# One array for the scan's h in place of two tiles, and the variance's clamp on VectorE

## The chip, the cores and the metric

The kernel runs on one core of a Trainium2 chip. The metric is the device time of one execution in microseconds (us). The engines are named as the profile names them: PE is TensorE, DVE is VectorE, ACT is ScalarE, POOL is GpSimd and SP is SyncE, which here only starts transfers.

## The reference

Eight images of 128 × 128 positions with 128 channels pass through two layers. Layer 0 is a linear attention block with a layer norm and a residual. Layer 1 projects to 2 × 256 channels (xb and z), runs a depthwise 3 × 3 convolution and a silu on xb, and then a selective scan with one state over the 16384 positions in four directions. What the change touches is the scan and the normalization behind it:

```python
delta = softplus(dt + dbias)                  # per channel and position
x_c   = exp(delta * A) * x_c + delta * u * Bt # the scan over positions
y     = x_c * Ct (+ u * D)                    # four directions are summed
yz    = (y0 + y1 + y2 + y3) * silu(z)
mu    = yz.mean(-1); xc = yz - mu
var   = (xc * xc).mean(-1)                    # over the 256 channels
out   = (gamma * xc / sqrt(var + 1e-05) + beta) @ Wout
```

## The kernel before, in words

The program has three stages: layer 0, the front of layer 1 (projection, convolution, the x projection), and the scan stage `layer1_scan`, which starts behind a barrier of all engines (L773). The change lies in the scan stage.

**Units.** The 256 channels lie as two halves c of 128 partitions. A scan of 16384 positions is cut in 16 chunks of 1024 (CH). A `Slot` is one direction of one output image; its number in the image is its *place*, 0 to 3. Eight images of four slots of 16 chunks make 512 units n = 0 to 511, and they run in that order. The sum of the directions, y, is one array in SBUF of 128 KB per partition.

**One unit.** PE makes delta's argument in PSUM (`delta`), ACT takes its softplus into `sp` (`soften`, L938) and the exponential into PSUM (`decay`, L942). POOL multiplies u by sp into h (`weigh`, L951, one for each half). DVE scans h in place (`scan`, L959 and L961), starting from the last column of the same half of the unit before. In the next step DVE multiplies h by the position's C, which PE has spread over the partitions in PSUM: `emit` writes y itself at place 0 (L979); at the other places it writes one 512-position half to PSUM (L989, L993), which `gather` (L1001) adds to y on DVE, and the other in place in h (L982), which `add` (L1009) adds to y on POOL.

**The buffers of h.** `weigh(n, 0)` takes a new tile of two halves from a pool with two buffers:

```python
hs[n] = wp.tile([P, NC2, CH], F32, name="h", bufs=2)
```

A new tile may be written only when everything that reads or writes the tile before it in that buffer, that of unit n − 2, is done. That takes in the second scan of unit n − 1, since `scan(n − 1, 1)` reads its starting column in h of unit n − 2.

**A leaving image.** When the four slots of image o are summed, its 16 pieces leave during the 16 units of place 0 of image o + 1 (after image 7, in 16 further steps without scans). I call these units *tails*. For a piece m: `gate` multiplies y by z (L1029; its half 1 on DVE where a piece left in the step before too, its half 0 on POOL); ACT squares it; PE sums both over the channels (`moments`), ACT copies the sums (`keep`), PE turns them to tokens (`to_tokens`), ACT squares the mean (`square_mean`, L1058); DVE subtracts (`variance`, L1062); POOL clamps and adds epsilon (`deviation`, L1066) and takes the power −1/2 (L1067), all on tiles of 128 × 8; PE multiplies the gated piece by Wout (`project`, L1074); DVE scales the product into r in eight instructions (`store`, L1080); and SP starts r's transfer to the output. Parts of the sum that came by way of DRAM are accumulated into y by transfers that POOL starts (`add_d`, L907, 1 MB each).

**What sets the order.** Within the stage each engine's instructions stand in the order in which `step(n)` (L1105 to L1189) issues them; `in_order` fixes it. Semaphores between the engines come from the tiles: who wrote and who read which region. In `step(n)`, the order on DVE is: emit and emit of unit n − 1, with the gate of half 1 between them, scan(n, 0), the store, scan(n, 1), variance. On POOL it is: weigh(n, 0), deviation, weigh(n, 1), the gate of half 0, add, add_d.

**Setup of the scan stage.** The weights of delta are split in three bf16 parts by `split3` (three casts and two subtractions on DVE) and written to DRAM, from where `Slot.weights` loads them for each slot in turn. The parts lie in a tile `w16` that borrows the buffers of h (tag "h", L782 to L794). It runs once for the weights (8 partitions) and once for the bias (1 partition).

Of the kernel before, what the change touches and what calls it, by code (L numbers as in the profile page):

```python
# [8 lines left out]
F32 = mybir.dt.float32  # L9
BF16 = mybir.dt.bfloat16  # L10
AF = mybir.ActivationFunctionType
ALU = mybir.AluOpType
# [4 lines left out]
P = 128  # L17
# [4 lines left out]
NC2 = 2  # L22
R = 8
K = 4
# [6 lines left out]
CH = 1024  # L31
# [3 lines left out]
EPS1 = 1e-5  # L35
# [5 lines left out]
def split3(eng, parts, x):  # L41

    for j in range(3):
        eng.tensor_copy(parts[j], x)
        if j < 2:
            eng.tensor_tensor(x, x, parts[j], ALU.subtract)
# [701 lines left out]
def layer1_scan(ctx: ExitStack, tc, ubs, xps, zs, gs, dtw, dtb, a_log, gamma, beta, w_out, out):  # L748
# [15 lines left out]
    nc = tc.nc  # L764
    const = ctx.enter_context(tc.tile_pool(name="l2c", bufs=1))
    big = ctx.enter_context(tc.tile_pool(name="l2b", bufs=1))
    wp = ctx.enter_context(tc.tile_pool(name="l2w", bufs=3))
# [14 lines left out]
    D2 = 2 * P  # L782
    wparts = dram.tile([3, R, K, D2], BF16, name="wparts")
    bparts = dram.tile([3, K, D2], BF16, name="bparts")
    for dst, src, rows in ((wparts, dtw.rearrange("k r d -> r k d"), R), (bparts, dtb.rearrange("o (k d) -> o k d", d=D2), 1)):
        x = wp.tile([rows, K, D2], F32, name="w32", tag="sp", bufs=2)
        nc.sync.dma_start(x, src)
        q = wp.tile([rows, 3, K, D2], BF16, name="w16", tag="h", bufs=2)
        split3(nc.vector, [q[:, j] for j in range(3)], x)
        for j in range(3):  # L790
            if rows == 1:
                nc.sync.dma_start(dst[j : j + 1], q[:, j])
            else:
                nc.sync.dma_start(dst[j], q[:, j])  # L794

# [49 lines left out]
        nc.vector.tensor_tensor(wg[:, c, :], wg[:, c, :], pb, ALU.subtract)  # L847

    y = big.tile([P, NC2, L], F32, name="y")
    yturn = y.rearrange("p c (w h) -> p c h w", h=H)  # L850

    class Slot:
# [49 lines left out]
    ubt, sp, da, hs = {}, {}, {}, {}  # L902
# [40 lines left out]

    def weigh(n, c):
        if c == 0:
            hs[n] = wp.tile([P, NC2, CH], F32, name="h", bufs=2)
        u, t, h = ubt.pop((n, c)), sp.pop((n, c)), hs[n][:, c, :]
        if units[n][0].permuted:
            u = u.rearrange("p (e h w) -> p h e w", e=2, w=W // 2)
            t, h = (v.rearrange("p (h e w) -> p h e w", e=2, w=W // 2) for v in (t, h))  # L950
        nc.gpsimd.tensor_tensor(h, u, t, ALU.mult)  # L951
# [108 lines left out]
    def variance(m):  # L1060
        rst[m] = rstd = sm.tile([P, GW, NC2], F32, name="rstd")
        nc.vector.tensor_tensor(rstd, pts.pop(m)[:, :, :, 1], mv.pop(m), ALU.subtract)  # L1062

    def deviation(m):
        rstd = rst[m]
        nc.gpsimd.tensor_scalar(rstd, rstd, 0.0, EPS1, ALU.max, ALU.add)  # L1066
        nc.gpsimd.tensor_tensor(rstd, rstd, half, ALU.pow)  # L1067

    def project(m, hf, bank):
# [20 lines left out]
    for o in range(B):  # L1090
        n = (o + 1) * K * NCH
# [13 lines left out]
    def step(n):  # L1105
# [22 lines left out]
        if live:  # L1128
            decay(n, 1)
            weigh(n, 0)  # L1130
            if n + 2 < N:
                load(n + 2, 0)
        if last:
            deviation(last[1])
        if live:
            weigh(n, 1)
            if n + 2 < N:
                load(n + 2, 1)
# [24 lines left out]
        if now:  # L1163
            variance(now[1])
# [42 lines left out]
@with_exitstack  # L1207
def tile_kernel(ctx: ExitStack, tc, a, out):
    dram = ctx.enter_context(tc.tile_pool(name="dram", bufs=1, space=DRAM))
    x1 = dram.tile([B, P, L], F32, name="x1")  # L1210
    ubs = dram.tile([B, 2, NC2, P, L], F32, name="ubs")
    xds = dram.tile([B, R + 2, L], F32, name="xds")
    xps = dram.tile([B, 2, 3, R + 2, L], BF16, name="xps")
    zs = dram.tile([B, NC2, P, L], F32, name="zs")
    gs = dram.tile([2, NC2, P, L], F32, name="gs")
    layer0(
        tc, a["x"], a["L0_conv_w_qkv"], a["L0_conv_w_out"], a["L0_conv_b_out"],
        a["L0_conv_gamma"], a["L0_conv_beta"], a["L1_conv_Win"], x1, zs,
    )
    layer1_front(  # L1220
        tc, x1, a["L1_conv_Win"], a["L1_conv_conv_w"], a["L1_conv_conv_b"], a["L1_conv_Wxproj"],
        a["L1_conv_D_param"], ubs, xds, xps, gs,
    )
    layer1_scan(
        tc, ubs, xps, zs, gs, a["L1_conv_dt_weight"], a["L1_conv_dt_bias"], a["L1_conv_A_log"],
        a["L1_conv_gamma"], a["L1_conv_beta"], a["L1_conv_Wout"], out,
    )
# [40 lines left out]
```

## Time and profile before

| | us |
|---|---|
| median of 3 executions (lowest, highest) | 9282.05 (9277.97, 9287.36) |
| the profiled execution | 9288.8 |
| its span, to which the profile refers | 9287.0 |
| scan stage: barrier, first scan, last scan | 4498.6, 4528.4, 9141.9 |
| busy in the span: DVE, POOL, ACT, PE | 7986.4, 7316.7, 7097.3, 6364.4 |
| busy on POOL in the scan stage: weigh L951, add L1009, gate L1029 | 2416.6, 1159.4, 329.7 |
| clamp L1066 and power L1067 on POOL, 128 each | 143.3, 212.9 |
| variance L1062 on DVE, 128 | 18.6 |

The profile is one execution. A group of instructions is a line, an engine, an operation and its operands (the names of the program, with shape and type), then how many there are, their busy time, the mean of one in ns, and the idle time in front of them with what ended most of it. A line of the timeline is start, duration, engine, line and operation; several alike in a row are taken together, and brackets hold the idle time ahead of it and what released it. Durations overlap a little at both ends: the next instruction can start some 0.06 to 0.1 us before the end of the one before it on its engine. A wait is put down to what came last.

### The profile page before, as it was taken

How to read it: one execution, taken by the hardware profiler on the slowest of the kernel's cores; microseconds unless marked ns; L12 is line 12 of the kernel's file. 1: busy time of each engine (PE TensorE's matmuls, PEld its weight loads, DVE VectorE, ACT ScalarE, POOL GpSimd, SP SyncE). 2: the span in 40 equal slices, each digit the busy share in tenths (PEclk: the TensorE clock that was granted, in tenths of full speed). 3: DMA queues.
4: the chain of work that ended last, by engine and by line, in shares of the span. 5: the costliest groups of instructions: out<-in, count | busy, mean ns of one | idle time of the engine just before them, and what ended most of it. 6: DMA issues, size and time to landing. Idle time of an engine off the chain costs nothing.

```text
span 9287.0 us, 91371 instructions
## 1 busy us (share of the span) xinstructions
PE 6364.4 (69%) x24512; PEld 3119.9 (34%) x24512; DVE 7986.4 (86%) x7953; ACT 7097.3 (76%) x8066; POOL 7316.7 (79%) x4684
## 2 busy tenths in 40 slices
PE   8899998988899999999334636346363463643636
PEld 5555555554333333333102304113041140311403
DVE  6667666774799999999799999999999999999996
ACT  5555555658789999999687787888888878888784
POOL 3446444564689988888599899999999989999897
PEclk9999999999999999999555657557575575755757
DMA  1322333223478788888658659577594775957757
GB/s 76 145 84 97 135 120 145 80 100 136 153 247 249 253 244 244 245 245 243 200 156 226 209 180 261 155 222 227 175 269 154 220 221 169 269 161 208 234 167 214
DMA packets 934770, 1750.67 MB, mean 189 GB/s; under 512 B 150228, under 2 KB 376148, under 8 KB 926064
## 3 DMA queue, kind: packets, MB, share of 16 engines
q1 hardware_dynamic: 873328, 1509.92, 48.0%
q0 software_dynamic: 60928, 234.90, 13.6%
q8 instruction: 200, 3.28, 0.1%
q14 instruction: 314, 2.57, 0.1%
HBM read 1052.36 MB, written 692.12 MB: 188 GB/s over the span
## 4 chain that ended last, share of the span: by engine, by line
DVE 36%; PE 5%; DMA 3%; issue 3%; POOL 2%; ACT 1%; DVEq 0%; SPq 0%; POOLq 0%; ACTq 0%
DVE h L961 10%; DVE h L959 10%; DVE y L1001 4%; DVE h L982 4%; DVE px L989 3%; PE px L1074 3%; DMA out<-r 3%; DVE r L1080 2%; DVE px L993 1%; POOL h L951 1%; PE pm L1042 1%; PE pq L1054 0%; PE pc L967 0%; POOL y L1009 0%; POOL z L1029 0%
## 5 line engine op out<-in xcount | busy, mean ns | idle before, releaser
L951 POOL TENSOR_TENSOR h<-ubt,sp 128x1024 f32<-128x1024 f32 x1024 | 2416.6, 2389 | 374.9 <-DMA rows<-xps 92.6
L934 PE MATMUL px<-rows,dtw 128*128 128x512 bf16 x2048 | 956.3, 566 | 2277.8 <-DVE y L1001 1073.2
L534 DVE SCALAR_TENSOR_TENSOR acc<-xb,cw,acc 128x1024 f32<-128x1024 f32 x1024 | 1320.3, 1289 | 133.6 <-ACT xb L502 89.8
L526 POOL TENSOR_TENSOR tap<-tap 128x1024 f32<-128x1024 f32 x512 | 1223.6, 2393 | 243.7 <-ACT tap L524 220.4
L938 ACT ACTIVATE sp<-px 128x1024 f32<-128x1024 f32 x1024 | 1046.7, 1024 | 436.4 <-PE px L934 413.8
L934 PEld LDWEIGHTS <-dtw 128*128 128x128 bf16 x2048 | 168.8, 110 | 3100.8 <-issue 1031.3
L961 DVE TENSOR_TENSOR_SCAN h<-px,h 128x1024 f32<-128x1024 f32 x512 | 1177.4, 2331 | 31.6 <-ACT px L942 15.4
L959 DVE TENSOR_TENSOR_SCAN h<-px,h 128x1024 f32<-128x1024 f32 x512 | 1178.1, 2330 | 22.4 <-POOL h L951 18.5
L1009 POOL TENSOR_TENSOR y<-y,h 128x512 f32<-128x512 f32 x768 | 1159.4, 1553 | 4.3 <-DVE h L982 4.3
L942 ACT ACTIVATE px<-sp,sa 128x1024 f32<-128x1024 f32 x1024 | 1110.4, 1109 | 6.1
L515 PE MATMUL acc<-xi,wt 128*128 128x512 f32 x2048 | 937.6, 600 | 53.6 <-ACT ures L539 53.6
L524 ACT ACTIVATE tap<-xb,cw 128x1024 f32<-128x1024 f32 x768 | 837.3, 1139 | 15.2 <-POOL xb L499 15.1
L282 POOL TENSOR_TENSOR q<-q,qs 128x512 f32<-128x512 f32 x256 | 271.6, 1061 | 697.0 <-DVE qs L281 697.0
L938 ACT ACT_TABLE_LOAD x512 | 656.9, 1283 | 164.6 <-PE px L934 162.7
L942 ACT ACT_TABLE_LOAD x512 | 656.9, 1283 | 9.2
L1074 PEld LDWEIGHTS px<-wg,z 128*128 128x128 f32 x4096 | 588.5, 229 | 113.3 <-issue 107.1
L1074 PE MATMUL px<-wg,z 128*128 128x128 f32 x4096 | 586.9, 312 | 0.0
L967 PE MATMUL pc<-rows,csel 128*128 128x512 bf16 x1024 | 520.0, 588 | 74.8 <-DVE rstd L1062 70.9
L515 PEld LDWEIGHTS acc<-xi,wt 128*128 128x128 f32 x2048 | 374.7, 189 | 573.9 <-issue 411.5
L488 PE MATMUL pxb<-xi,wi 128*128 128x512 f32 x1024 | 495.6, 606 | 2.1 <-ACT xb L497 2.1
L298 ACT ACTIVATE sq<-o 128x512 f32<-128x512 f32 x256 | 161.2, 630 | 420.3 <-DVE o L296 419.1
L1001 DVE TENSOR_TENSOR y<-y,px 128x1024 f32<-128x1024 f32 x384 | 468.5, 1220 | 14.4
(153 smaller groups left out, 15037.9 us busy)
## 6 DMA issues: line engine op xcount, KB each, us to landing
ubt<-ubs SPq DMA_DIRECT2D x1024, 512.0 KB
zs<-z SPq DMA_DIRECT2D x512, 256.0 KB
ubs<-ures SPq DMA_DIRECT2D x256, 512.0 KB
ubs<-turned SPq DMA_DIRECT2D x256, 512.0 KB
z<-zs SPq DMA_DIRECT2D x256, 512.0 KB
y<-gs POOLq DMA_DIRECT2D x128, 1024.0 KB, 10.3
gs<-du POOLq DMA_DIRECT2D x96, 1024.0 KB, 8.6
rows<-xps SPq DMA_DIRECT2D x1536, 60.0 KB
```

The lines of the kernel that those rows point to most:

```text
L515: nc.tensor.matmul(acc[:, s, :], wt[:, j, c, :], x, start=(j == 0), stop=(j == len(ON_PE) - 1))
L526: nc.gpsimd.tensor_tensor(sums[n, c], sums[n, c], t, ALU.add)
L534: nc.vector.scalar_tensor_tensor(acc, at(n, c, *d), weight(n, c, *d), acc, ALU.mult, ALU.add)
L934: nc.tensor.matmul(p[:, hf * 512 : hf * 512 + 512], sl.dw[:, c * P : c * P + P], src, start=True, stop=True)
L938: nc.scalar.activation(t, da[n, c], AF.Softplus)
L942: nc.scalar.activation(da[n, c], sp[n, c], AF.Exp, scale=sa[:, sl.s, c : c + 1])
L951: nc.gpsimd.tensor_tensor(h, u, t, ALU.mult)
L959: nc.vector.tensor_tensor_scan(e[:, ::-1], x[:, ::-1], e[:, ::-1], start, ALU.mult, ALU.add)
L961: nc.vector.tensor_tensor_scan(e, x, e, start, ALU.mult, ALU.add)
L1001: nc.vector.tensor_tensor(v, v, ts.pop(n), ALU.add)
L1009: nc.gpsimd.tensor_tensor(v[:, c], v[:, c], h[:, c], ALU.add)
L1074: nc.tensor.matmul(po[:, w, :], z[:, c, w * H : w * H + H], wg[:, c, :], start=(c == 0), stop=(c == NC2 - 1))
```

## The change

It has three parts. First, h is no longer a tile for each unit: one array of two times two halves is set up once, and unit n uses the part n % 2. It is never released or taken again, so the engines are ordered by the regions that they read and write, half by half. It takes the same 16 KB per partition. Second, the clamp (maximum with 0, plus epsilon, on 128 × 8 fp32 in place) goes from POOL's `deviation` to DVE's `variance`, right behind the subtraction that writes its operand. Third, since h has no pool buffers to lend any more, the setup's `w16` tiles borrow those of u (tag "ub", four buffers of 4 KB per partition) and hold two of the four k at a time: `split3` runs twice for each of the two arrays, on half of the elements, and its parts are stored with twelve transfers instead of six.

```diff
--- before.py
+++ after.py
@@ -785,13 +785,14 @@
     for dst, src, rows in ((wparts, dtw.rearrange("k r d -> r k d"), R), (bparts, dtb.rearrange("o (k d) -> o k d", d=D2), 1)):
         x = wp.tile([rows, K, D2], F32, name="w32", tag="sp", bufs=2)
         nc.sync.dma_start(x, src)
-        q = wp.tile([rows, 3, K, D2], BF16, name="w16", tag="h", bufs=2)
-        split3(nc.vector, [q[:, j] for j in range(3)], x)
-        for j in range(3):
-            if rows == 1:
-                nc.sync.dma_start(dst[j : j + 1], q[:, j])
-            else:
-                nc.sync.dma_start(dst[j], q[:, j])
+        for k in range(0, K, 2):
+            q = wp.tile([rows, 3, 2, D2], BF16, name="w16", tag="ub", bufs=4)
+            split3(nc.vector, [q[:, j] for j in range(3)], x[:, k : k + 2])
+            for j in range(3):
+                if rows == 1:
+                    nc.sync.dma_start(dst[j : j + 1, k : k + 2], q[:, j])
+                else:
+                    nc.sync.dma_start(dst[j, :, k : k + 2], q[:, j])
 
 
 
@@ -847,6 +848,7 @@
         nc.vector.tensor_tensor(wg[:, c, :], wg[:, c, :], pb, ALU.subtract)
 
     y = big.tile([P, NC2, L], F32, name="y")
+    hring = big.tile([P, 2, NC2, CH], F32, name="h")
     yturn = y.rearrange("p c (w h) -> p c h w", h=H)
 
     class Slot:
@@ -943,7 +945,7 @@
 
     def weigh(n, c):
         if c == 0:
-            hs[n] = wp.tile([P, NC2, CH], F32, name="h", bufs=2)
+            hs[n] = hring[:, n % 2]
         u, t, h = ubt.pop((n, c)), sp.pop((n, c)), hs[n][:, c, :]
         if units[n][0].permuted:
             u = u.rearrange("p (e h w) -> p h e w", e=2, w=W // 2)
@@ -1060,10 +1062,10 @@
     def variance(m):
         rst[m] = rstd = sm.tile([P, GW, NC2], F32, name="rstd")
         nc.vector.tensor_tensor(rstd, pts.pop(m)[:, :, :, 1], mv.pop(m), ALU.subtract)
+        nc.vector.tensor_scalar(rstd, rstd, 0.0, EPS1, ALU.max, ALU.add)
 
     def deviation(m):
         rstd = rst[m]
-        nc.gpsimd.tensor_scalar(rstd, rstd, 0.0, EPS1, ALU.max, ALU.add)
         nc.gpsimd.tensor_tensor(rstd, rstd, half, ALU.pow)
 
     def project(m, hf, bank):
```

## The prediction

> **What bounds the kernel now.** I read the engine shares first, then the windows of the scan stage (L773 at 4498 us to the end), then its timeline, groups and waits. The whole change lies in that stage. The windows give each engine's busy time, with the transfer share second to last; the first lies in a slot in which no image leaves, the second in one in which an image leaves.
>
> ```profile
> core 0: us, PE busy (x) PEld busy (x) DVE busy (x) ACT busy (x) POOL busy (x), PEclk, DMA share, GB/s
> 5300.00:5370.00 70.00, 24.67 (x52) 4.80 (x51) 68.75 (x44) 58.00 (x52) 66.72 (x35) 0.50 0.48 150
> 6255.00:6395.00 140.00, 109.14 (x770) 81.70 (x770) 138.99 (x172) 116.40 (x126) 128.74 (x68) 0.93 0.93 290
> ```
>
> VectorE is busy for 98% and 99% of them; its work and what delays it set the time. From start to start of the scans of channel half 0, a unit (one chunk) takes by place: place 0 of image 0, 114.6 us for 16 units (7.17 each); places 1 and 2, 131.5 (8.22 each); place 3, 135.2, of which the last two units take 9.5 and 10.6; place 0 of images 1 to 7, where the image before leaves ("tails"), 195.6, 187.8, 179.0, 182.4, 192.5, 181.4, 188.3, with 11.3 as the usual unit. One tail unit, from the timeline (start, duration, engine):
>
> ```profile
> 8011.01 0.13 DVE L1062 TENSOR_TENSOR rstd<-pq,mv 128x8 f32<-128x8 f32 x1
> 8011.19 1.22 DVE L979 TENSOR_TENSOR y<-h,pc 128x1024 f32<-128x1024 f32 x1
> 8011.23 2.36 POOL L951 TENSOR_TENSOR h<-ubt,sp 128x1024 f32<-128x1024 f32 x1
> 8012.33 2.34 DVE L1029 TENSOR_TENSOR z<-y,z 128x1024 f32<-128x1024 f32 x1
> 8013.57 1.21 POOL L1066 TENSOR_SCALAR rstd<-rstd 128x8 f32<-128x8 f32 x1
> ...
> 8014.87 1.66 POOL L1067 TENSOR_TENSOR rstd<-rstd,half 128x8 f32<-128x8 f32 x1
> ```
>
> The gate L1029 takes 2.34 and ends at 8014.67, 1.08 after weigh L951 (8013.59). In the last 16 units, with no weigh beside it, it takes 1.22. So it is held until the weigh is over. The clamp L1066, on eight elements, is in turn held for 1.21 until the gate is done; at 5051.64, alone, it took 0.27. A tail unit on VectorE is, start to start, emit 1.13 + gate 2.34 − 0.06 overlap + emit 1.13 + scan 2.26 + store 2.05 + scan 2.26 + L1062 0.18 = 11.29.
>
> At each slot boundary it is POOL that is late, since the second-half adds and the gates meet there:
>
> ```profile
> 5030.59 4.65 DVE L961 TENSOR_TENSOR_SCAN h<-px,h 128x1024 f32<-128x1024 f32 x2 [1.23 <-POOL h L951]
> ...
> 5041.20 4.60 DVE L959 TENSOR_TENSOR_SCAN h<-px,h 128x1024 f32<-128x1024 f32 x2 [2.24 <-POOL h L951]
> ```
>
> The waits (us in total, times, longest) say what all such stalls are worth, and how often the store waits for its buffer's transfer:
>
> ```profile
> DVE r L1080 <- DMA out<-r: 80.7, 32, 6.4
> ...
> DVE h L959 <- POOL h L951: 18.5, 12, 2.2
> ...
> DVE h L961 <- POOL h L951: 15.0, 10, 2.2
> ```
>
> **What the skill says.** "SBUF — State Buffer", section "Who interferes with whom", says that VectorE and GpSimd share a port pair as an exclusive lock; a VectorE instruction with two SBUF inputs contends with a GpSimd instruction that reads SBUF, and a tensor_scalar that can enter a two-port mode contends too. The trace agrees for the gate (2.34 against 1.22). "VectorE: DVE Perf Modes", section "Mode 2×_2P — use both read ports for one tensor", makes that mode tensor_scalar territory, so the moved clamp, fp32 in SBUF, may be held where L1062, which reads PSUM, is not. The trace has a tensor_scalar of the clamp's very size:
>
> ```profile
> L779 DVE TENSOR_SCALAR sa<-sa 128x8 f32<-128x8 f32 x1 | 0.6, 570 | 0.4 <-ACT sa L778 0.4
> L1062 DVE TENSOR_TENSOR rstd<-pq,mv 128x8 f32<-128x8 f32 x128 | 18.6, 145 | 33.1 <-ACT mv L1058 32.9
> ```
>
> L779 took 570 ns and ended when POOL's MEMSET L805 ended. L214 took 0.56 at 145.14 beside POOL's L327, and 0.28 alone. These point to a lock, but the first could be coincidence. The pow L1067 holds nothing: VectorE's instructions with two SBUF inputs ran at full speed beside the pow of layer 0.
>
> **The change part by part.**
>
> 1. *One array for h.* Today weigh(n,0) takes the buffer of h(n−2), which is free only when scan(n−1,1) has read its start value there. In steady slots it starts 0.13 to 0.24 after that scan's end (5309.60, weigh at 5309.84) and POOL idles 0.36 to 0.38 a unit. With regions alone, half 0 needs only scan(n−1,0), some 2.3 us earlier. By place:
>    - Places 1 to 3: VectorE's 8.22 is a sum of its own work (1.27 + 1.13 + 1.13 + scans 4.69), with POOL at about 7.9 beside it. An earlier weigh gains nothing within: 0.
>    - First slot: scan 0 at 4592.77 starts when the weigh ends (4592.71), and VectorE idles 2.8 in 16 units. That goes: −2.6.
>    - Boundaries: seven images with stalls of 1.23 + 2.24 + 1.14 = 4.6. POOL enters with 0.37 of idle saved per unit, but gets no further ahead than about 1.5, since the add waits for emit's L982 in the same unit. I let 1.9 of 4.6 go per boundary, and 1.3 at unit 511: −14.6. Late next is the same weigh, by the remaining 2.7.
>    - Tails: the weigh now starts when sp is ready, 6.46 after the gate's end in most units, instead of after the second scan at about 7.7.
>
> 2. *The clamp moves.* POOL loses 128 × 1.12 = 143 us. VectorE gains 128 instructions. Alone, the price is between 0.15 (the issue spacing of small instructions; L1062 takes 0.145) and 0.2, since it reads what L1062 has just written. Held, it lasts until the weigh's end. Its value is read only by the pow and the stores, but behind it on VectorE stand emit, gate, emit and scan. If the weigh starts at 6.46 and the clamp comes at 7.7 + 0.18, I take it as held: next gate end = 6.46 + 0.06 + weigh 2.36 + clamp 0.17 + emit 1.13 + gate 1.08 = 11.26 against 11.29. The hold has moved from the gate to the clamp, and the tail gains 0.03 in some 91 units: −2.7. In about 30 units sp comes later, 6.6 to 7.2, because PE's project runs at 418 ns a matmul instead of 275; each costs up to 0.4, about half of them absorbed ahead of a store stall: +6. After the roughly 25 store stalls ('out<-r'), POOL is ahead, the weigh is over, and the gate and clamp run alone; today the gate takes 1.65 there: 25 × 0.4 = −10. In the last 16 units the store waits for its transfer, which covers the clamp's shorter path: 0, bounds ±2.
>
> 3. *Setup in pairs of k.* Twenty split instructions instead of ten, at half the size, and 12 store DMAs on SP's queue instead of 6, ahead of the weight loads (4512 to 4518) on which the first scan (4528.4) depends. The casts take 0.67 and the subtracts 1.20 at full size; halves cost about the same in sum. The first weights are of k in the first pair, which could let them start sooner. I take +1.5, bounds −3 and +5. The "ub" buffers that it borrows are loaded later in SP's own order: no new wait.
>
> Sum: −2.6 − 14.6 − 2.7 + 6 − 10 + 1.5 = −22. The profiled execution took 9288.8 (span 9287.0), 6.8 above the median of the runs, 9282.05, by 0.07%; I take the difference off the median: **9260**.
>
> **The rivals.**
>
> *The clamp is not held* (too small for a two-port mode, or it takes the lock first). Then the tail unit is bound by ScalarE's own loop: its instructions start to start are 9.24 and it waits 1.29 for the moments, 10.53 in all; VectorE's would be 10.25. 13 units × 7 images × 0.76 = −69 on top of the −10 to −20 of boundaries and first slot. But tails stand at 0.84 to 0.95 DMA share, and the add_d transfers of 1 MB plus store stalls of about 54 us in tails would take some back: −26 to −69 remain. In all −45 to −89, about 9225. For it: L1062 is never held; against: L779, L214.
>
> *Slower.* The early weigh does not come, or comes just before the clamp, so that only the price of the moved clamp is left. In 112 tail units VectorE then has 0.17 to 0.2 more ahead of emit and gate: 22 if nothing hides it. If the weigh starts soon before the clamp, after a late sp (7.2 or more), the clamp's hold pushes emit and gate fully: 7.2 + 4.80 = 12.0 against 11.29, so +0.7; in half of 91 units, +32. It decides from sp at 6.5 after the gate's end: beyond that, every 0.1 is 0.1. With boundaries helping a little: +20 to +45, about 9302. For it: a third of the units already lie beyond that point; against: the mean over units is near it.
>
> *Nothing moves.* The tails are DMA-bound (0.93 share in the window above), the stalls reappear as longer store waits, and boundaries move half a microsecond: −6 to 0, about 9278. The same time comes if the weigh's early start is not granted and the clamp's price hides in the gate's wait of 1.1.
>
> **How the numbers follow.** The hold moves: 0.50. Its own range is 9238 to 9290, from sp's lateness (±15), boundaries gaining between 0 and all 34, and setup −3 to +5. Clamp free: 0.26. Slower: 0.16. Nothing moves: 0.08. A difference of 0.2% (18.6 us) is about what a measurement here can tell from none. The first case lies at its threshold, 9263.5: some six tenths of it is beyond (0.31), 0.18 within, 0.01 above. The free clamp gives 0.25 to faster and 0.01 to an unforeseen loss. That makes 0.56 faster; 0.18 + 0.08 = 0.26 same; 0.16 + 0.02 = 0.18 slower. The range 9200 to 9300 leaves out the far end of the free clamp and the slow half of the slower case.
>
> **What would show it.** Right: L1029 in tails falls to about 1.2, and the clamp's row on VectorE has a mean of 1 us or more, not 0.2; weighs start before the second scan's end; POOL's L951 stalls at boundaries fall from 33 to under 20 us; tail units stay near 11.3. The free clamp: its mean is under 0.25 and tail units are 10.5 to 10.8. Slower: tail units of 11.5 to 12, weighs starting between the second scan and the clamp. Wrong altogether: steady units other than 8.22, or a first scan shifted by more than 5 us.

## The result, and the profile after

The changed kernel takes 9319.15 us (median of 6 executions, 9310.59 to 9333.57) against 9284.03 for the kernel before beside it: a ratio of 1.0038, 95% interval 1.0026 to 1.0051. It is slower by 35 us; 9260 was predicted, in a range of 9200 to 9300. Its profiled execution took 9322.88 us, span 9321.1, so 34.1 us more than the profiled span of before. Lines behind the setup have moved by two: weigh is L953, the gate L1031, the subtraction L1064, the moved clamp L1065, the store L1082.

From the starts of the scans of half 0 in the two traces, the 34 us come to (the last scan is the last one of half 0):

| part | before | after | difference |
|---|---|---|---|
| first scan (setup) | 4528.4 | 4528.1 | −0.3 |
| place 0 of image 0 | 114.6 | 113.8 | −0.8 |
| places 1 and 2, all images | 2121.1 | 2121.8 | +0.7 |
| place 3, to the last scan | 1070.8 | 1055.3 | −15.5 |
| seven tails | 1307.0 | 1358.9 | +51.9 |
| last scan to the end | 145.1 | 143.3 | −1.8 |

The waits of VectorE (us in total, times, longest) show the boundaries: POOL's weigh made it wait for 33.5 us before and for 10.7 now. The waits for the output transfer, 80.7 in all before, are 72.1; but within the seven tails alone they rose from 45.4 us (24 times) to 56.4 (38 times).

```profile
DVE r L1082 <- DMA out<-r: 72.1, 43, 6.6
...
DVE h L961 <- POOL h L953: 6.0, 4, 1.5
DVE h L963 <- POOL h L953: 4.7, 3, 1.6
```

The groups of the scan stage on VectorE (busy, mean ns | idle before) show the hold in its new place. The gate is down from 2123 ns (first line, the kernel before) to 1214. The clamp takes 1174, while the subtraction ahead of it, of the same size, takes 149.

```profile
L1029 DVE TENSOR_TENSOR z<-y,z 128x1024 f32<-128x1024 f32 x120 | 254.7, 2123 | 0.0
```

```profile
L1065 DVE TENSOR_SCALAR rstd<-rstd 128x8 f32<-128x8 f32 x128 | 150.3, 1174 | 4.4
L1031 DVE TENSOR_TENSOR z<-y,z 128x1024 f32<-128x1024 f32 x120 | 145.7, 1214 | 0.0
L1064 DVE TENSOR_TENSOR rstd<-pq,mv 128x8 f32<-128x8 f32 x128 | 19.1, 149 | 44.9 <-ACT mv L1060 44.7
```

In the seven tails, VectorE's gates took 236.4 us before; its gates and clamps take 127.3 and 147.6 now, 38.5 more together. Two neighbouring tail units of the changed kernel in the timeline (start, duration, engine):

```profile
6359.19 2.35 POOL L953 TENSOR_TENSOR h<-ubt,sp 128x1024 f32<-128x1024 f32 x1 [2.36 <-ACT mv L1060]
6359.20 0.17 DVE L1064 TENSOR_TENSOR rstd<-pq,mv 128x8 f32<-128x8 f32 x1 [0.41 <-ACT mv L1060]
6359.40 2.17 DVE L1065 TENSOR_SCALAR rstd<-rstd 128x8 f32<-128x8 f32 x1
6361.49 1.21 DVE L981 TENSOR_TENSOR y<-h,pc 128x1024 f32<-128x1024 f32 x1
...
6362.62 1.21 DVE L1031 TENSOR_TENSOR z<-y,z 128x1024 f32<-128x1024 f32 x1
...
6370.37 2.35 POOL L953 TENSOR_TENSOR h<-ubt,sp 128x1024 f32<-128x1024 f32 x1 [1.97 <-ACT sp L940]
6371.46 0.13 DVE L1064 TENSOR_TENSOR rstd<-pq,mv 128x8 f32<-128x8 f32 x1
6371.62 1.12 DVE L1065 TENSOR_SCALAR rstd<-rstd 128x8 f32<-128x8 f32 x1
```

In the second the weigh starts early, at 6370.37, before the second scan is over, and ends at 6372.72; the clamp is held until then, 1.12 us. In the first the softplus came late (it ended at 6359.10; the bracket names the ScalarE instruction behind it), the weigh starts only at 6359.19, just ahead of the clamp, and the clamp is held for the weigh's whole length, 2.17 us. Emit and gate follow, then everything of the next unit. From one gate's end to the next there are 14 tail units in each tail, 98 in all. In 69 of them the clamp is held, and each of the 69 ends within 0.05 us of the weigh's end.

A tail of both kernels in windows (second to last: the transfer share; before it the granted clock of PE): before first, then after, where the same tail is 18 us longer.

```profile
6226.00:6404.00 178.00, 137.72 (x961) 101.21 (x954) 175.37 (x215) 145.94 (x157) 162.71 (x86) 0.92 0.90 278
```

```profile
6226.00:6422.00 196.00, 160.33 (x968) 120.19 (x961) 180.45 (x231) 145.55 (x157) 152.85 (x72) 0.80 0.87 253
```

### The profile page after: what moved, and what is told of

Its sections match the earlier page's. It is cut to its first block, busy times and chain, and to the rows that moved or that the text cites. A ratio compares the mean times of both kernels' runs of the same rounds, so it can differ in the third digit from the quotient of the medians.

```text
span 9321.1 us, 91655 instructions
## 1 busy us (share of the span) xinstructions
PE 6394.8 (69%) x24512; PEld 3147.8 (34%) x24512; DVE 8021.3 (86%) x8091; ACT 7099.0 (76%) x8066; POOL 7222.6 (77%) x4556
## 4 chain that ended last, share of the span: by engine, by line
DVE 37%; PE 5%; DMA 5%; issue 3%; ACT 1%; POOL 0%; DVEq 0%; SPq 0%; ACTq 0%; POOLq 0%
DVE h L963 11%; DVE h L961 10%; DMA out<-r 5%; DVE y L1003 5%; DVE h L984 4%; DVE px L991 3%; PE px L1076 3%; DVE r L1082 2%; DVE px L995 2%; PE pm L1044 1%; DVE y L981 1%; PE pq L1056 0%; ACT px L944 0%; PE pc L969 0%; ACT L940 0%
## 5 line engine op out<-in xcount | busy, mean ns | idle before, releaser
L953 POOL TENSOR_TENSOR h<-ubt,sp 128x1024 f32<-128x1024 f32 x1024 | 2487.7, 2488 | 325.0 <-ACT sp L940 186.6
L940 ACT ACTIVATE sp<-px 128x1024 f32<-128x1024 f32 x1024 | 1046.2, 1024 | 425.6 <-PE px L936 410.9
L963 DVE TENSOR_TENSOR_SCAN h<-px,h 128x1024 f32<-128x1024 f32 x512 | 1176.2, 2330 | 22.4 <-ACT px L944 15.7
L1076 PEld LDWEIGHTS px<-wg,z 128*128 128x128 f32 x4096 | 609.5, 236 | 114.6 <-issue 108.4
L1076 PE MATMUL px<-wg,z 128*128 128x128 f32 x4096 | 607.9, 320 | 0.0
```

Of the source, the lines that this page charges most:

```text
L940: nc.scalar.activation(t, da[n, c], AF.Softplus)
L963: nc.vector.tensor_tensor_scan(e, x, e, start, ALU.mult, ALU.add)
L1076: nc.tensor.matmul(po[:, w, :], z[:, c, w * H : w * H + H], wg[:, c, :], start=(c == 0), stop=(c == NC2 - 1))
```

## The experiments

All ratios are to the kernel before, run on the same chip. Differences between variants are worked out from the ratios, at 9284 us.

**1. The change in halves.** `ring_only` puts the clamp back on POOL:

```diff
     def variance(m):
-        nc.vector.tensor_scalar(rstd, rstd, 0.0, EPS1, ALU.max, ALU.add)
...
     def deviation(m):
+        nc.gpsimd.tensor_scalar(rstd, rstd, 0.0, EPS1, ALU.max, ALU.add)
```

> One array for h and the setup in pairs, with the clamp left on POOL. Three theories of the 35 us: (H) the early weigh holds the moved clamp on VectorE (mean 1.17 us), and the hold passes to the gate and to ScalarE; (L) the early weigh itself is the loss, because it now depends on a softplus that PE's slow projects make late; (D) VectorE pays for 128 instructions more. H expects the gate to fall to about 1.2 us with the clamp on POOL at 0.3, tail units of 10.5 to 11.2, and 9200 to 9255 us. L expects tails as after the whole change, 12.2 a unit, and 9300 to 9320. D expects the boundaries' gain alone, about 9265.

Measured: 9287.53, ratio 1.0001 (0.9993 to 1.0009). None of the three theories gave this time. The loss is gone, so it needs the moved clamp, and L falls. But H's gain is not there either.

`move_only` is the kernel before with the clamp's line in `variance`, behind the subtraction, and not in `deviation`.

> The clamp on VectorE, with the tiles and the setup of before. H expects that the weigh still starts 0.13 after the second scan, at about 7.84 after the gate's end, so that the clamp (issued at 7.79) gets in just ahead of it: 0.17 us, not held, the gate still held to 2.3, tail units of 11.3 to 11.45, and 9280 to 9300 us. L expects the time of before, 9284. D expects most of the 35 us here, 9305 to 9320.

Measured: 9306.34, ratio 1.0026 (1.0015 to 1.0037). In time this lies at the low end of D, 6 above H's range. The timeline shows H's place for it, and the cleanest picture of the lock, the same instruction twice:

```profile
6325.43 2.35 POOL L951 TENSOR_TENSOR h<-ubt,sp 128x1024 f32<-128x1024 f32 x1 [3.00 <-issue]
6325.84 0.17 DVE L1062 TENSOR_TENSOR rstd<-pq,mv 128x8 f32<-128x8 f32 x1 [0.56 <-ACT mv L1058]
6326.04 1.76 DVE L1063 TENSOR_SCALAR rstd<-rstd 128x8 f32<-128x8 f32 x1
...
6339.35 0.17 DVE L1063 TENSOR_SCALAR rstd<-rstd 128x8 f32<-128x8 f32 x1
6339.40 2.37 POOL L951 TENSOR_TENSOR h<-ubt,sp 128x1024 f32<-128x1024 f32 x1 [4.78 <-ACT mv L1058]
```

Started 0.05 us ahead of the weigh, the clamp takes 0.17; started behind it, 1.76, until the weigh's end. Of the 98 tail units it was held in 26, and 61 took 11.29 as before. In its seven tails the clamps take 76 us, and the gates only 24 less than before.

**2. The clamp not held.** `clamp_from_psum` keeps the change, but the clamp does not read SBUF:

```diff
-        nc.vector.tensor_tensor(rstd, pts.pop(m)[:, :, :, 1], mv.pop(m), ALU.subtract)
-        nc.vector.tensor_scalar(rstd, rstd, 0.0, EPS1, ALU.max, ALU.add)
+        v = pts.pop(m)[:, :, :, 1]
+        nc.vector.tensor_tensor(v, v, mv.pop(m), ALU.subtract)
+        nc.vector.tensor_scalar(rstd, v, 0.0, EPS1, ALU.max, ALU.add)
```

> The whole change, but the variance is subtracted in place in PSUM, and VectorE's clamp reads it there and writes SBUF. H: a clamp that does not read SBUF is not held by the weigh, 0.2 us as L1062 is; gate 1.2; tail units 10.4 to 11.2 (ScalarE's loop of 10.5 is next); 9195 to 9250 us. L expects 9300 to 9320 as after the whole change. D expects the same as L, since VectorE has the same instructions.

`clamp_after_emit` issues VectorE's clamp in the next step behind the first `emit`, ahead of the gate.

> The whole change, but VectorE's clamp stands behind the first emit of the next step, ahead of the gate, and reads SBUF as in the change. H: in units whose softplus comes at 6.46 the weigh is over at 8.89, the emit at 8.9, so the clamp is not held; with a later softplus it is held for up to 1.2. Tail units 10.3 to 11.8, 9215 to 9280 us. L and D expect 9300 to 9320.

Measured: 9303.88, ratio 1.0022 (1.0013 to 1.0031), and 9289.02, ratio 1.0008 (1.0002 to 1.0015). The mechanism came out and the times did not. From PSUM the clamp takes 167 ns in the mean and is held in no unit, and behind the emit it is held for over 0.5 us in 46 units instead of 69; 30 and 32 of the 98 tail units fell below 11.05, to 10.2 in the shortest. But others grew: 26 in each took over 13. The waits of the store point to the reason, first `ring_only`, then `clamp_from_psum`:

```profile
DVE r L1082 <- DMA out<-r: 98.5, 47, 5.5
```

```profile
DVE r L1083 <- DMA out<-r: 118.0, 54, 6.0
```

Faster engines ran into the output transfer: 80.7 us of stalls before, 98.5 and 118.0 here (117.9 in `clamp_after_emit`). That gave a new theory, T: the engines' gain is real, and the transfers take it back.

**3. Fewer transfers.** Four kernels without the accumulating transfers y<-gs:

```diff
-        if n in summed:
-            add_d(*summed[n])
```

> The kernel before, leaving out the accumulating transfers of add_d (128 of 1 MB, y<-gs), that is, one term of u times D in the sum. It is the base for the next three. Theory T: in ring_only and clamp_from_psum the engines' tail unit did fall to 10.2 to 10.9, but the output transfers could not follow, and the store's wait for its buffer took the gain back (wait 80.7 before, 98.5 and 118.0 there). Rival F: those short units come only because a stall before them let POOL and PE get ahead, and without stalls the engines settle at 11.3 as before. Expected by both: stalls of out<-r under 10 us, tails 11.29 a unit, 179 each, about 9225 us.

> One array for h with the clamp on POOL, without y<-gs. T expects tail units of 10.2 to 10.7, 164 to 172 a tail, and 9120 to 9180 us, 50 to 100 below the base. F expects tails of 178 or more, and a difference to the base of the boundaries alone, 10 to 20 us.

> The whole change without y<-gs. If the held clamp is the cause of the whole change's loss against ring_only, then with few stalls its tail units stay between 11.2 and 12.7 (a unit whose softplus is on time, then one whose softplus is late by 0.6 to 1.6), 186 to 192 a tail: 40 to 80 us above the base. If transfers were the cause, it comes to the base or below, 9205 to 9225.

> The whole change with the clamp reading PSUM, without y<-gs. T expects it within 10 us of ring_no_gs, tail units of 10.3 to 10.8. F expects the base less 10 to 20.

| without y<-gs | us | ratio (95%) | tails, us |
|---|---|---|---|
| before | 9211.25 | 0.9918 (0.9903 to 0.9934) | 1251.8 |
| ring_only | 9133.36 | 0.9835 (0.9817 to 0.9852) | 1191.0 |
| after | 9247.06 | 0.9956 (0.9941 to 0.9972) | 1300.9 |
| clamp_from_psum | 9136.43 | 0.9837 (0.9819 to 0.9854) | |

T holds and F falls, with the base 14 us lower than expected; `after_no_gs` is 35 above the base, 5 short of its range. The array alone gains 77 us against the base, the whole change loses 35, and the same change with a clamp that is not held gains 75. The held clamp costs 112 us here against the clamp on POOL (0.9956 − 0.9835 = 0.0121) and 110 against the clamp from PSUM, and VectorE's extra instruction nothing that can be seen. D falls. A unit of `ring_no_gs` in the timeline:

```profile
6236.92 2.36 POOL L953 TENSOR_TENSOR h<-ubt,sp 128x1024 f32<-128x1024 f32 x1 [0.47 <-ACT sp L940]
6237.63 0.14 DVE L1064 TENSOR_TENSOR rstd<-pq,mv 128x8 f32<-128x8 f32 x1
6237.81 1.22 DVE L981 TENSOR_TENSOR y<-h,pc 128x1024 f32<-128x1024 f32 x1
6238.95 1.41 DVE L1031 TENSOR_TENSOR z<-y,z 128x1024 f32<-128x1024 f32 x1
6239.25 1.22 POOL L1068 TENSOR_SCALAR rstd<-rstd 128x8 f32<-128x8 f32 x1
```

The weigh is early, the emit beside it takes its usual 1.22, the gate is held for 0.2 only, and the clamp waits for the gate on POOL, where nobody needs it soon: 10.44 from gate to gate.

In `after_no_gs` 61 of 98 units take 11.17, 16 take 11.6 to 11.8 and 21 take 12.6 to 12.7. The late ones follow PE. Where PE's project takes 3.73 us, the softplus ends 6.46 after the gate and the unit is on time. In the 16 the project takes mostly 5.36 and the softplus ends at about 7.05; in the 21 it takes 6.1 and the softplus ends at 8.0; all of this lateness is in the unit. After a unit of 12.7, whose clamp was held for 2.17, the gate itself comes later and a project of 5.36 is on time again, so that in every second tail units of 11.17 and 12.7 alternate. These tails of 190.8 differ from those of 182 in PE's granted clock, third from last in these windows:

```profile
5613.00:5803.00 190.00, 159.25 (x945) 120.88 (x962) 183.59 (x231) 147.40 (x160) 144.22 (x65) 0.78 0.71 218
6187.00:6369.00 182.00, 125.54 (x886) 88.53 (x901) 178.53 (x222) 148.21 (x157) 149.81 (x69) 0.91 0.73 228
```

The Trainium skill, "TensorE: Matmul & The Clock Gate", section "🔬 Part 1: The HAM clock gate (the "warmup" mystery)", has PE's clock follow its recent activity, halved or full; project times of 3.73 and 5.36 to 6.1 us at mean granted clocks of 0.91 and 0.78 agree in kind. Why the clock is lower in every second tail was not tried.

**4. More buffers.** Six buffers for r instead of two, paid for by four for z instead of six, with the fetch of z moved to the end of the step, and that of an image's third piece from 20 units ahead to 2:

```diff
-        r = wp.tile([P, GW, P], F32, name="r", bufs=2)
+        r = wp.tile([P, GW, P], F32, name="r", bufs=6)
...
-            zt[m, hf] = z = wp.tile([P, NC2, GN], F32, name="z", bufs=6)
+            zt[m, hf] = z = wp.tile([P, NC2, GN], F32, name="z", bufs=4)
```

> One array for h, the clamp on POOL, the computation whole; six buffers for the output r instead of two, paid for by four for z instead of six (the fetch moves to the end of the step). If what swallowed ring_only's gain was the store waiting for a late output transfer, more buffers let DVE run on: out<-r waits fall from 98 to under 20 us, tail units to 10.4 to 11, tails 170 to 182, and 9150 to 9230 us. If the transfer engines' throughput as such is the bound, the wait only moves (to z, ubt or rows) and the time stays at 9260 to 9290.

> The kernel before with the same six buffers for r and four for z. By the first theory tails go to 179 (held gate, no stalls): 9225 to 9245 us. By the second, 9260 to 9290.

> The whole change with six buffers for r and four for z. By the first theory the held clamp shows fully, as without y<-gs: tail units 11.2 to 12.7, 183 to 192 a tail, 9260 to 9290 us, so 30 to 60 above before_r6 and 80 to 130 above ring_r6. By the second, all three lie within 30 us of each other.

Measured: 9293.84 (1.0012, 1.0003 to 1.0021), 9319.94 (1.0041, 1.0026 to 1.0056) and 9333.98 (1.0060, 1.0043 to 1.0076). The first theory's times fall, and so do the second's (9260 to 9290, all three within 30 us). VectorE's wait for out<-r is down to 2.2 us in `ring_r6`, and POOL now waits for z instead:

```profile
POOL z L1031 <- DMA z<-zs: 130.3, 45, 10.3
```

This does not show throughput alone to be the bound, since z's own lead was cut as well.

**5. The same transfers, spread.** The 16 y<-gs of an image begin in place 3 and end in the tail. In the kernels named gs_earlier the last one starts 19 units after the first instead of 23, and five lie in the tail instead of seven:

```diff
-            summed[n - NCH + 3 + (3 * j + 1) // 2] = e
+            summed[n - NCH + 3 + (5 * j + 1) // 4] = e
```

In those named gs_unit the last term is `j`: one transfer a unit, the last 15 units after the first, and three in the tail.

> ring_only with the 16 y<-gs transfers of an image spread over 19 units instead of 23, so that five lie in the tail instead of seven or eight. It tells whether the tails' loss goes with the number of those transfers in them. Theory T: some 5 us of transfer time less in each tail, fewer out<-r stalls, 5 to 8 us a tail, less up to 3 where POOL's issue (1.25 us each) makes place 3 later: 9240 to 9275. If stalls don't depend on them: 9285 to 9300.

> The kernel before with the y<-gs transfers spread over 19 units instead of 23. If the transfers set the tails and the early weigh has room only when they are thinner, before gains less than ring_only did: tails 179 to 184 (held gate at 11.29 is the floor), POOL later at the boundaries, 9255 to 9280 us. If the earlier transfers alone made ring_only's 50 us, it falls to 9230 to 9245.

> The whole change with the same spread. The hold predicts tails of 186 to 192, 9280 to 9305 us, 45 to 70 above ring_gs_earlier. If the transfers were the loss, 9235 to 9255.

> The whole change with the clamp from PSUM and the same spread. The hold predicts it near ring_gs_earlier, 9230 to 9255 us, since the clamp is not held; the two small instructions on VectorE (0.37 a unit) are hidden behind the transfers. Were it the added instruction or the clamp's place and not the hold, it would lie with after_gs_earlier, above 9280.

> ring_only with one y<-gs a unit, so that 13 of 16 lie in place 3. Tails lose three more transfers' time (to 172 to 178), but in place 3 POOL has 7.9 + 1.25 a unit against VectorE's 8.22, so it falls behind by up to 0.9 a unit in 13 units and seven or eight images: places 3 longer by 5 to 12 each. 9200 to 9250 us.

> The kernel before with one y<-gs a unit. The held gate keeps tails at 179 or more (11.29 a unit), and POOL, which also waits 0.36 a unit for the second scan, is later in place 3: 9245 to 9275 us, 60 to 90 above ring_gs_unit. If the transfers alone made the gain, 9185 to 9215.

> The whole change with one y<-gs a unit. The hold predicts tail units between 11.2 and 12.7 again, 182 to 190 a tail, and 9255 to 9290 us, 70 to 105 above ring_gs_unit; so no better than before_gs_unit. If the transfers were the loss, 9185 to 9215.

| y<-gs, first to last | before | ring_only | after | clamp_from_psum |
|---|---|---|---|---|
| 23 units | 9284 | 9287.53, 1.0001 | 9319.15, 1.0038 | 9303.88, 1.0022 |
| 19 units | 9265.70, 0.9981 (0.9975 to 0.9988) | 9234.36, 0.9948 (0.9934 to 0.9963) | 9285.33, 1.0001 (0.9992 to 1.0009) | 9258.35, 0.9969 (0.9958 to 0.9980) |
| 15 units | 9256.01, 0.9970 (0.9961 to 0.9980) | 9184.41, 0.9894 (0.9879 to 0.9909) | 9279.60, 0.9994 (0.9985 to 1.0004) | |

Four of the seven came within the ranges that T or the hold gave; `ring_gs_earlier` was 6 us and `ring_gs_unit` 16 us below its range, `psum_gs_earlier` 3 us above. The rivals of each (the transfers alone made the gain; the transfers were the loss) fall. The computation is whole in all of them. Moving y<-gs forward to one a unit is worth 28 us to the kernel before, whose held gate keeps 78 of its 98 units at 11.3, and 99 to `ring_only`. The whole change against `ring_only` costs 34, 49 and 93 us in the three rows: the less the transfers press, the more of the hold is seen. Against `clamp_from_psum`, which leaves out the hold and keeps the rest, it costs 15 and 30 in the first two; so of the 35 us, that comparison gives some 15 to the hold alone. `ring_gs_unit` is the fastest version, 1.06% below before. Its place 3 is longer than `ring_only`'s by 14 us over all images (1069.2 against 1055.1), where 5 to 12 for each had been expected; its tails are shorter by 100 (1216.7 against 1316.9); its stalls on out are down from 98.5:

```profile
DVE r L1082 <- DMA out<-r: 24.3, 8, 6.4
```

## Why the prediction was wrong

**What came as predicted.** The clamp is held by the early weigh (1174 ns in the mean; 1 us or more was the sign named), the gate is down to 1.2 and the weigh starts before the second scan's end. The on-time tail unit is 11.17 where the sum said 11.26. Setup gave −0.3 where +1.5 was taken, within its bounds; the last 16 units −1.8, within ±2. Steady units stayed at 8.22.

**Right in size, by luck in part.** At the boundaries POOL's stalls and with them place 3 gave 15.5 where 14.6 was summed. But what is late next is not the same weigh: in the first tail unit VectorE waits for ScalarE's squared mean. In `ring_only` place 3 is shorter by 15.7, and the stretch from a tail's first scan to its first gate's end is longer by 16.1 over the seven tails, so that the gain is gone again.

**The step that failed is the tails' term**: −2.7 + 6 − 10 = −7 was summed, +52 measured. Of the 52, 21 lie in the 98 units, 24.5 between a tail's first scan and its first gate's end, and 6.3 behind its last gate. Two parts of the term were mis-sized and one was not in it.

- *Late softplus, +6.* It took about 30 units to be late, 6.6 to 7.2 after the gate's end, and so by at most 0.4 each. The trace of before has more: 55 of the 98 units are later than 6.6, 30 later than 7.1 and 11 later than 7.8. Lateness up to 1.4 cost nothing there, because the weigh began at 7.84 anyway. In the changed kernel 41 units have the softplus later than 7.1 and 28 later than 7.8, and the lateness is paid in full, once as the weigh's start and then through the clamp: the 63 units without a wait for the output exceed 11.17 by 49 us in sum, as much as their softplus ends behind 6.46 (48 us). Before, 78 such units exceed 11.28 by 20. Without y<-gs, where little else disturbs, the 98 units average 11.60 against 11.29, which is 30 us. The "Slower" rival had this very price (0.1 for each 0.1 beyond 6.5) and came to 9302; what was wrong was to give it 0.16 on the ground that the mean lay near the break-even. A mean near a one-sided threshold is itself a loss.
- *Stalled units, −10.* Units that wait for the output were to become shorter because gate and clamp run alone. They are shorter (12.70 us in the mean instead of 13.80), but there are 35 of them instead of 20, and what they take beyond an on-time unit is 53 us where it was 50. `ring_only` and `clamp_from_psum` show the same more strongly: where y<-gs is in the tails, shorter work there lengthens the waits for the output.
- *The first tail unit, at nothing.* It takes 12.7 in all seven tails (10.4 before), the next one 11.2 to 12.4 (12.3 to 12.5). From the first scan to the first gate's end it is 11.6 instead of 8.1, each time. VectorE waits longer for the squared mean, and then the clamp is held by a weigh that starts with it. Before, then after:

```profile
5046.02 0.17 DVE L1062 TENSOR_TENSOR rstd<-pq,mv 128x8 f32<-128x8 f32 x1 [0.23 <-ACT mv L1058]
...
5047.27 2.04 DVE L1029 TENSOR_TENSOR z<-y,z 128x1024 f32<-128x1024 f32 x1
```

```profile
5044.52 0.17 DVE L1064 TENSOR_TENSOR rstd<-pq,mv 128x8 f32<-128x8 f32 x1 [1.70 <-ACT mv L1060]
5044.55 2.99 POOL L953 TENSOR_TENSOR h<-ubt,sp 128x1024 f32<-128x1024 f32 x1
5044.72 2.86 DVE L1065 TENSOR_SCALAR rstd<-rstd 128x8 f32<-128x8 f32 x1
...
5048.62 1.21 DVE L1031 TENSOR_TENSOR z<-y,z 128x1024 f32<-128x1024 f32 x1
```

The first slot's −2.6 came to −0.8: its idle time of 2.8 us did not go, so the late weigh was not its cause. Two readings: the 54 us of store stalls put in the tails are 45.4 in the trace; and the MEMSET beside L779 is L806, not L805. That L779 ended with a MEMSET was no coincidence: in all 20 traces of this case it takes between 0.37 and 1.00 us and ends within 0.03 us of the end of one.

**The rivals.** "The clamp is not held" was given −45 to −89. `clamp_from_psum` made it so and was slower than before by 20. Its engine part was right in size (10.44 in most units of `ring_no_gs`, 10.53 reckoned); the allowance for the transfers was not: they took all of it, until y<-gs was spread, and then the array with the clamp on POOL came to 98 below the kernel before, of which 28 are the spread's own. "Nothing moves" had the transfers as the bound, which is what `ring_only` shows, but not for the kernel with the held clamp.

**Open.** `clamp_from_psum` is above `ring_only` by 20 us with the transfers of before and with the earlier ones, but level without y<-gs; no run separates its two small instructions from the pow, which takes 2.38 us there in the mean in place of 1.69. Whether the slow projects come from the longer units, or the reverse, was not tried.

## What to carry to other kernels

When an early start is won for one engine, look at what then overlaps: an instruction on eight elements per partition that shares a lock with a 2.4 us one costs 0.17 ahead of it and up to 2.2 behind it (2.86 behind the longer weigh of a first tail unit), so keep it on the engine that nobody waits for, or give it operands outside the lock. Lateness that a wait hides has to be read as a distribution before that wait is removed, since every value beyond the new start is paid. A stall that goes at a boundary is a gain only if the first unit behind the boundary doesn't give it back. Where a stage has both a tight engine loop and transfers at 0.9 of their engines, try the loop's gain with transfers taken out of the stage: here the same edit (the array with the clamp on POOL) gave 0 with them and 77 without.

## What the runs showed of the hardware

- A tensor_scalar on 128 × 8 fp32 in SBUF on VectorE takes 0.17 us alone and 1.76 to 2.17 when a GpSimd multiply of 128 × 1024 began 0.2 to 0.6 before it; from PSUM it takes 0.167 in the mean and was held in none of 98 units. The Trainium skill, "SBUF — State Buffer", section "Who interferes with whom", has VectorE and GpSimd share a port pair as an exclusive lock, which a tensor_scalar in a two-port mode needs; these runs add that an instruction on eight elements per partition is held until the other's end.
- The pow on GpSimd is held by the gate too when that starts first: 2.64 us at 6341.70 in `move_only`, beside the gate, against 1.67 at 6327.88. The reverse was not seen: where the pow is about 1 us under way when the gate starts, 105 times in the changed kernel, the gate takes 1.21 to 1.22.
